# A graph layer with a mixture of experts on one core: when two late experts' weights, two sets of scatters and a few transposes are issued

## The chip, the cores and the metric

The kernel runs on one core of one Trainium2 chip. The metric is device time in microseconds (us) of one launch, as the median of several runs. The core has five engines that run side by side, each with its own queue of instructions in a fixed order: TensorE (PE in the profile, with PEld for its weight loads), VectorE (DVE), ScalarE (ACT), GpSimd (POOL) and SyncE (SP). An engine waits with the instruction at the head of its queue, and everything behind that instruction waits with it. DMAs are issued from the queues of SP, ACT and POOL and run on 16 DMA engines that all three share.

## What is computed

`x` is 3125 nodes of 256 floats, `src` and `dst` are 100,000 edges sorted by `dst`. All numbers are float32.

```
xn  = layernorm(x)
e   = relu((xn[dst] - xn[src]) @ theta.T + theta_b + xn[src] @ phi.T + phi_b)
gnn = segment_max(e, dst)                       # 0 where a node has no edge
mix = linear attention of xn over 8 heads, projected, + bias
x   = x + gnn + mix
z   = layernorm(layernorm(x))
top 2 of 8 experts per node, by softmax(z' @ Wr);  expert: gelu(z @ W1 + b1) @ W2 + b2
out = x + w0 * expert0(z) + w1 * expert1(z)
```

An expert has two matrices, 256 by 1024 and 1024 by 256, 1 MB each.

## The kernel before, in words

**Edges.** The message of an edge is a maximum over rows of a table `b_d` in DRAM. The edges lie in 128 runs of 782. POOL gathers 128 rows at a time (`gather`, L107, tile `g`), 755 of these steps, and DVE folds each into a running maximum (`fold`, L366). Eight steps share a window `g` of the pool `wide`, which has `WN` = 5 buffers. SP stores each folded window to `s_d`. The order of steps is cut into four groups of node tiles: group 0 has tiles 12 to 24, group 1 tiles 5 to 11, group 2 tiles 1 to 4, group 3 tile 0.

**A group** (`group`, L1128) starts when its last fold is in the queue: `carry` links the 128 runs, `routed_tile` finishes the gnn sum, both norms and the router for each node tile, `dispatch` works out each node's slots in the experts' buffers and scatters the nodes' rows there (`xs_d`, L114, two scatters a tile). Then the `Stream` (`go`, L720) takes the experts' lots: load rows (`rows`), transpose (`turn`, L698), scale (`scaled`, L709, tile `xe`), and a unit of eight steps: `hp` (L615), GELU into `hT` (L617), and, one unit behind, `yp` (L639). Group 0 has 16 units, groups 1 and 2 have eight each. Weights come in four parts of 512 KB on ACT's queue, three experts' worth of buffers `w`.

**Group 3** is one tile, and all its 128 nodes go through all eight experts (`dense_tile`, L786), in the order 5, 6, 7, 0, 1, 2, 3, 4. The first three experts' weights are still held by the stream. Expert 0 is loaded into parts of `xn_lo` (SP, in `first_maxima`) and `xn_hi` (ACT's queue, at the end of `go`). Expert 1 goes into two buffers of `wide` (SP, in `combines`). Experts 2, 3 and 4 take the freed buffers `w` (ACT's queue, `next_dense`, L1199, 2 MB in one DMA), issued at step 1 of the third, fourth and fifth expert. DVE makes the scaled input `xe` of the next expert (L802) at step 1 of each expert, and adds each expert's result (L829).

**The combines** (`combine`, L1295; `finale`, L1334) bring the experts' rows of groups 0, 1 and 2 back: POOL gathers `ys_d` into a buffer of `wide` (two gathers a tile, four tiles), DVE adds them with two operations a tile (L1308), and SP stores `out`. There are seven: four tiles from each of tiles 12, 16, 20, one tile 24, then 5 (four), 9 (three) and 1 (four). The text calls them c12, c16, c20, c24, c5, c9, c1. A buffer of `wide` can be used again when its `out` store has landed.

**The maxima** (`first_maxima`, L1207) find, for the four first nodes, the maximum over all nodes that have an edge to them: DVE, L1228, 25 steps beside the folds, then PE transposes (L1235) and two more small stages (L1242, `last_ends`, L1264 and L1275). **The last fold** of group 3 is followed on PE by `pick_ends` (L1287) and `carry` (L373, L384), then by `routed_tile(0)` (L445 to L495).

**What sets the order.** The order on PE, DVE, ACT and SP is the order in which Python emits it, written by generators: `yield 3` means that the task goes on three ticks later. A tick is one POOL instruction (`TICK` = 1.25 us); each issue on POOL moves the clock by one. A stream unit's steps follow a second count, `clock["pe"]`, of the work that PE has been given. An engine runs ahead of the ticks when its operands are there, so ticks fix orders, not times.

Of the kernel before, what the change touches and what calls it, by code (L numbers as in the profile page):

```python
# [19 lines left out]
P = 128  # L20
# [12 lines left out]
FC = H // P  # L33
# [34 lines left out]
def gps_layer(ctx: ExitStack, tc: tile.TileContext, x, src, dst, thetaT, phiT, gbias, wq, wkvT,  # L68
# [583 lines left out]
    class Stream:  # L652
# [67 lines left out]
        def go(self):  # L720
            units = Units(self.ps, self.act)
            u, q = 0, -1
            for k in range(3):
                self.next_w(k)
                yield 25
            while True:
                if u == len(self.lots):

                    for _ in units.last():
                        yield room()  # L730
                    units.behind = None
                    if not self.open:
                        break
                    if G - 3 in self.through:
                        nc.scalar.activation(table, eps, AF.Sqrt)
                    while u == len(self.lots):
                        yield 1
                if ("xe", u) not in self.held:
                    self.rows(u // 2)
                    yield 8  # L740
                    self.turn(u)
                    yield 2
                    self.scaled(u)
                    yield 2
                g, e, h = self.lots[u]
                v = u // 2
                if u % 2 == 0:
                    ys = self.at(2) if v % 2 else self.act.tile([P, 4, D], F32, name="ys", bufs=1)

                def done(r, yp, u=u, ys=ys):  # L750
                    g, e, h = self.lots[u]
                    n = self.half(u)
                    nc.tensor.matmul(yp[0:n, :], ident[0:E, e:e + 1].to_broadcast([E, n]), b2_sb, start=False, stop=True)  # L753
                    nc.scalar.copy(ys[0:n, u % 2 * 2 + r, :], yp[0:n, :])
                    if u % 2 and r:
                        move(nc.scalar, self.two(ys_d, u // 2), self.as_two(ys, u // 2))
                        if u + 1 == len(self.lots) or self.lots[u + 1][0] != g:
                            self.through.add(g)

                between = {4: lambda: self.turn(u + 1), 6: lambda: self.scaled(u + 1)}  # L760
                if u % 2 == 0:
                    between[1] = lambda: self.rows(v + 1)
                if h == 0:
                    q += 1
                    if q:
                        between[7] = lambda: (self.next_w(q + 2, self.parts), self.part())
                at_step = dict(between)
                for f in (0, 2, 5):
                    between[f] = lambda f=f: (self.part(), at_step.get(f, int)())
                w1t, w2t = self.held["w", q]  # L770
                for _ in units.run(e, w1t, self.held["xe", u], w2t, done, between, 2, self.half(u)):
                    yield room()
                u += 1
            for k in range(3):
                dense_w[DENSE[k]] = self.held["w", q - 2 + k]
            dense_half(0, 1, xn_hi[:, 0:FC, :].rearrange("p i d -> p (i d)"), nc.scalar)
            clock["through"] = True

    def spread(pool, i, pick):
# [6 lines left out]
    def dense_tile(act, ps, mm, i, shared, w, next_w, order=range(E), ready=None):  # L786


        tr = mm.tile([P, 2, P], F32, name="mm")
        for c in range(2):  # L790
            nc.tensor.transpose(tr[:, c, :], xn2(i)[:, c * P:(c + 1) * P], ident)
        xT = act.tile([P, 2, P], F32, name="xT", bufs=1)
        nc.vector.tensor_copy(xT, tr)
        held = {}
        yield 1

        def scaled(k):
            if k < E:
                e = order[k]
                held["xe", e] = act.tile([P, 2, ROWS], F32, name="xe")  # L800
                for c in range(2):
                    nc.vector.tensor_scalar(held["xe", e][:, c, 0:P], xT[:, c, :], sm[:, c, e:e + 1],  # L802
                                            sm[:, 2 + c, e:e + 1], op0=OP.mult, op1=OP.add)

        while ready is not None and "through" not in ready:
            yield 1
        scaled(0)
        o = act.tile([P, D], F32, name="o", bufs=1)

        def second_bias():  # L810

            bt_p = mm.tile([E, P], F32, name="mm")
            nc.tensor.transpose(bt_p, full, ident)
            bt = act.tile([E, P], F32, name="bt", bufs=1)
            nc.vector.tensor_copy(bt, bt_p)
            held["bt"] = bt

        def add_bias():
            bb = mm.tile([P, D], F32, name="mm")
            nc.tensor.matmul(bb, held["bt"], b2_sb, start=True, stop=True)  # L820
            nc.vector.tensor_add(x_sb[:, i, :], x_sb[:, i, :], bb)

        units = Units(ps, act, True)
        for k, e in enumerate(order):
            def done(r, yp, k=k, e=e):
                if k == 0:
                    nc.vector.tensor_scalar(o, yp, full[:, e:e + 1], None, op0=OP.mult)
                else:
                    nc.vector.scalar_tensor_tensor(o, yp, full[:, e:e + 1], o, op0=OP.mult, op1=OP.add)  # L829

            between = {1: lambda k=k: scaled(k + 1)}
            if k == 1:
                between.update({3: second_bias, 5: add_bias})
            if k > 1:
                between[1] = lambda k=k: (next_w(k - 2), scaled(k + 1))
            while k == 1 and not shared:
                yield 1
            for _ in units.run(e, w[e][0], held["xe", e], w[e][1], done, between, 1, P):
                yield 1
        nc.vector.tensor_add(o, o, x_sb[:, i, :])  # L840
        for _ in units.last():
            yield 1
        n = rows_in(i)
        move(nc.sync, out[i * P:i * P + n, :], o[0:n])
# [263 lines left out]
    def dispatch(g, half, i0, i1, top, top_i, taken):  # L1108

        ro = at_hand["route"]  # L1110
        while not all(i in routed for i in range(i0, i1)) or len(taken) < half:
            yield 1
        yield 1
        made = []
        at = i0 - GROUPS[g][0]
        rest = shares(ro, i0, i1, top[:, at:at + i1 - i0, :], top_i[:, at:at + i1 - i0, :], made,
                      15 if g == G - 2 and half == 0 else 0)
        start(rest, clock["now"] + next(rest))
        yield from slots(ro, mm, g, half, i0, i1, made[0], taken)
        yield 1 if g == G - 2 else 9  # L1120
        put = []
        for i in range(i0, i1):
            n = rows_in(i)
            for k in range(2):
                put.append((xs_d[g][:], slot_i[0:n, k, i:i + 1], xn2(i)[0:n]))
        scatter(*put)
# [80 lines left out]
    def first_maxima():  # L1207
# [11 lines left out]
        for i in range(NT):  # L1219
# [4 lines left out]
            for k in range(FIRST):  # L1224
# [4 lines left out]
                                                   op1=OP.max)  # L1229
                yield 1.4  # L1230
        most = at_hand["first"].tile([P, 2, FIRST], F32, name="most")
        for c in range(2):
            tr = mm.tile([P, FIRST, P], F32, name="mm")
            for k in range(FIRST):
                nc.tensor.transpose(tr[:, k, :], of_k[:, k, c * P:(c + 1) * P], ident)  # L1235
            on_pe(1.2)
            yield 4
            nc.vector.tensor_reduce(most[:, c, :], tr, AX.X, OP.max)
            yield 2
# [75 lines left out]
    def combines(g):  # L1315

        i0, i1 = GROUPS[g]
        whole = i1 - (i1 == NT)
        for i in range(i0, whole, W // 2):
            nt = min(W // 2, whole - i)  # L1320
            start(combine(g, i, nt))
            yield 2 * nt
            if g == 0 and i == i0 + W // 2:

                while "shared" not in clock:
                    yield 1
                yield 6
                for k in range(2):
                    dense_half(1, k, wide.tile([P, HALF], F32, name="g"))
        if i1 == NT:  # L1330
            start(combine(g, NT - 1, 1))
            yield 2

    def finale():  # L1334

        for g in range(G - 1):
            while g not in at_hand["ffn"].through:
                yield 1
            yield from combines(g)

    def starts(g):

# [7 lines left out]
    def folding():  # L1350

        for g in range(G):
            last = None
            rows = s_d[1 + P * COL[g]:1 + P * COL[g + 1], :].rearrange("(p t) d -> p t d", t=STEPS[g])
            for w, (t0, n) in enumerate(starts(g)):
# [6 lines left out]
                if g < G - 1 or t0 + n < STEPS[g]:  # L1362
                    move(nc.sync, rows[:, t0:t0 + n, :], wins[g, w][:, 0:n, :])
            clock["last"] = last
            if g == 0:
                open_late()
            start(group(g))
# [193 lines left out]
```

## Time and profile before

| | us |
|---|---|
| median of 3 runs (lowest, highest) | 1219.15 (1218.51, 1221.02) |
| the profiled execution, its own time | 1217.85 |
| its span, first to last instruction | 1216.0 |
| mean granted TensorE clock | 0.856 of full speed |
| busy: PE, DVE, ACT, POOL | 938.2, 678.6, 326.0, 885.8 |

Some stretches, from the view of busy time by stage (busy us of each engine; granted clock; DMA engines' mean busy share):

| stretch, us | what runs | PE | DVE | POOL | clock | DMA |
|---|---|---|---|---|---|---|
| 550 to 600 | group 0's units | 50.00 | 18.45 | 38.12 | 1.00 | 0.82 |
| 850 to 900 | group 1's units | 50.00 | 26.14 | 38.41 | 1.00 | 1.01 |
| 950 to 1000 | group 2's routing | 22.84 | 38.87 | 37.77 | 0.50 | 0.55 |
| 1050 to 1100 | group 2's units | 48.02 | 21.14 | 37.95 | 0.97 | 1.02 |
| 1100 to 1150 | last fold, tile 0 | 48.84 | 25.00 | 34.90 | 1.00 | 0.65 |
| 1150 to 1216 | dense experts, combines | 52.39 | 24.26 | 24.06 | 0.93 | 0.63 |

A line of a timeline gives start, duration, engine, line, operation, output from input with its shape, a count, and in brackets the idle time before it and what ended that time. "issue" there means that the profile shows no engine or DMA that was waited for.

### The profile page before, as it was taken

How to read it: one execution, taken by the hardware profiler on the slowest of the kernel's cores; microseconds unless marked ns; L12 is line 12 of the kernel's file. 1: busy time of each engine (PE TensorE's matmuls, PEld its weight loads, DVE VectorE, ACT ScalarE, POOL GpSimd, SP SyncE). 2: the span in 40 equal slices, each digit the busy share in tenths (PEclk: the TensorE clock that was granted, in tenths of full speed). 3: DMA queues.
4: the chain of work that ended last, by engine and by line, in shares of the span. 5: the costliest groups of instructions: out<-in, count | busy, mean ns of one | idle time of the engine just before them, and what ended most of it. 6: DMA issues, size and time to landing. Idle time of an engine off the chain costs nothing.

```text
span 1216.0 us, 13364 instructions
## 1 busy us (share of the span) xinstructions
PE 938.2 (77%) x3929; PEld 670.4 (55%) x3929; DVE 678.6 (56%) x1998; ACT 326.0 (27%) x762; POOL 885.8 (73%) x911
## 2 busy tenths in 40 slices
PE   6556866645923548689999999979999527999986
PEld 5323433323311323258888887868887315777786
DVE  7669866685336772433333587455546764433633
ACT  4212222210101222133333343323332112332331
POOL 6677777777777777777777777777777777776733
PEclk9778888866965557889999999989999557999998
DMA  8668877666685664467888787689999658998683
GB/s 280 214 200 277 302 253 242 227 227 207 207 292 194 239 235 157 156 238 258 285 307 310 251 284 271 227 308 356 380 370 367 219 191 305 375 387 301 201 338 94
DMA packets 103928, 320.13 MB, mean 263 GB/s; under 512 B 20897, under 2 KB 44186, under 8 KB 92325
## 3 DMA queue, kind: packets, MB, share of 16 engines
q0 software_dynamic: 44032, 119.73, 31.5%
q1 hardware_dynamic: 29724, 115.08, 24.4%
q10 hardware_dynamic: 30089, 84.36, 19.3%
q8 instruction: 33, 0.54, 0.2%
q14 instruction: 50, 0.41, 0.1%
HBM read 192.05 MB, written 127.04 MB: 262 GB/s over the span
## 4 chain that ended last, share of the span: by engine, by line
PE 43%; DMA 5%; issue 4%; POOL 3%; DVE 2%; ACT 1%; ACTq 0%; POOLq 0%; DVEq 0%; SPq 0%
PE yp L639 18%; PE hp L615 18%; PE yp L753 3%; POOL g L107 2%; DMA w<-in_w 2%; DMA g<-b_d,srcI 2%; PE trf L698 1%; POOL xs_d L114 1%; DMA xn_lo<-b_d 1%; PE am L445 1%; DVE g L366 1%; PE mm L491 0%; DMA xn_hi<-xs_d 0%; DMA r<-s_d,end_i 0%; PE mm L403 0%
## 5 line engine op out<-in xcount | busy, mean ns | idle before, releaser
L107 POOL DMA_INDIRECT g<-b_d,srcI x755 | 738.2, 978 | 238.4 <-issue 203.8
L366 DVE SCALAR_TENSOR_TENSOR g<-g,cut 128x256 f32<-128x256 f32 x751 | 363.5, 484 | 356.8 <-DMA g<-b_d,srcI 339.0
L639 PE MATMUL yp<-w,hT 128*128 128x256 f32 (+1 forms) x1120 | 296.8, 387 | 0.0
L615 PE MATMUL hp<-xe,w 128*128 128x256 f32 (+2 forms) x1216 | 285.9, 361 | 11.5 <-issue 5.6
L615 PEld LDWEIGHTS hp<-xe,w 128*128 128x128 f32 x1216 | 216.7, 196 | 49.2 <-issue 18.0
L617 ACT ACTIVATE hT<-hp,sm 128x256 f32<-128x256 f32 (+2 forms) x320 | 140.2, 439 | 335.8 <-PE hp L615 335.3
L639 PEld LDWEIGHTS yp<-w,hT 128*128 128x128 f32 (+1 forms) x1120 | 201.1, 185 | 39.7 <-issue 12.4
L1012 PE MATMUL kv<-wkv,xn_lo 128*128 128x512 f32 x96 | 54.5, 720 | 38.0 <-DVE kn L1030 24.1
L1012 PE MATMUL kv<-wkv,xn_hi 128*128 128x512 f32 x104 | 59.3, 724 | 30.9 <-DVE kn L1030 30.2
L107 POOL DMA_INDIRECT g<-ys_d,from_i x48 | 46.1, 960 | 32.4 <-DVE g L1308 18.7
L445 PE MATMUL am<-cr,oh 128*128 128x257 f32 x86 | 37.3, 560 | 27.8 <-DVE r L450 19.9
L1012 PEld LDWEIGHTS kv<-wkv,xn_lo 128*128 128x128 f32 x96 | 21.1, 231 | 63.8 <-issue 60.3
L1012 PEld LDWEIGHTS kv<-wkv,xn_hi 128*128 128x128 f32 x104 | 22.8, 230 | 58.3 <-issue 55.6
L1228 DVE SCALAR_TENSOR_TENSOR xn_lo<-xn_lo,no_edge 128x256 f32<-128x256 f32 x96 | 45.9, 479 | 16.1 <-DMA xn_lo<-b_d 16.1
L401 PE MATMUL mm<-bias,ones 1*128 1x512 f32 x50 | 32.4, 731 | 16.2 <-ACT x_sb L408 12.9
L753 PE MATMUL yp<-b_sb,ident 8*128 8x256 f32 (+1 forms) x128 | 43.9, 422 | 0.0
L1016 ACT ACTIVATE sq<-kv 128x1024 f32<-128x1024 f32 x25 | 25.5, 1019 | 59.3 <-PE kv L1012 59.3
L445 PEld LDWEIGHTS am<-cr,oh 128*128 128x128 f32 x86 | 20.3, 267 | 37.1 <-issue 24.9
L709 ACT ACTIVATE xe<-trf,sm 128x256 f32<-128x256 f32 (+1 forms) x64 | 31.3, 544 | 27.6 <-PE trf L698 27.6
L1035 PEld LDWEIGHTS dots_p<-kn,vn 128*128 128x128 f32 x200 | 26.9, 199 | 19.0 <-issue 19.0
L1024 ACT ACTIVATE rsk<-var,eps 128x16 f32<-128x16 f32 x25 | 7.7, 308 | 110.7 <-DVE var L1021 110.7
L698 PE MATMUL trf<-ident,xn_hi 128*128 128x128 f32 (+1 forms) x128 | 19.2, 275 | 22.2 <-DMA xn_hi<-xs_d 22.2
(285 smaller groups left out, 991.1 us busy)
## 6 DMA issues: line engine op xcount, KB each, us to landing
s_d<-g SPq DMA_DIRECT2D x80, 1024.0 KB
w<-in_w ACTq DMA_DIRECT2D x84, 512.0 KB
w<-in_w ACTq DMA_DIRECT2D x6, 2048.0 KB
g<-b_d,srcI POOLq DMA_INDIRECT x755, 4.5
s_d<-g SPq DMA_DIRECT2D x13, 896.0 KB
xn_hi<-xs_d ACTq DMA_DIRECT2D x12, 512.0 KB
xs_d<-zero ACTq DMA_DIRECT2D x8, 512.0 KB
b_d<-bt SPq DMA_DIRECT2D x5, 640.0 KB
```

What stands on the lines that cost most here:

```text
L107: got = nc.gpsimd.indirect_dma_start(out=to, out_offset=None, in_=table, in_offset=row_index(index))
L366: nc.vector.scalar_tensor_tensor(g[:, j, :], last, cut[:, t:t + 1], g[:, j, :], op0=OP.add, op1=OP.max)
L401: nc.tensor.matmul(am, ones[0:1, :], bias, start=True, stop=False)
L445: nc.tensor.matmul(r2, picks[k], carried[g], start=(k == 0), stop=(k == len(slices) - 1))
L615: nc.tensor.matmul(hp[:, 0:n], w1t[:, c, f, :], xe[:, c, 0:n], start=(c == 0), stop=(c == 1))
L617: nc.scalar.activation(hT[f][:, 0:n], hp[:, 0:n], AF.Gelu, bias=sm[:, 4 + f, e:e + 1])
L639: nc.tensor.matmul(yp[r][0:part, :], hT[q][:, r * part:(r + 1) * part], w2t[:, q, :], start=(q == 0), stop=(q == FC - 1 and self.whole))
L698: nc.tensor.transpose(tr[:, c, r * n:(r + 1) * n], self.held["xs", u // 2][0:n, u % 2 * 2 + r, c * P:(c + 1) * P], ident[0:n, 0:n])
L709: nc.scalar.activation(xe[:, c, 0:n], self.held["tr", u][:, c, 0:n], AF.Identity, bias=sm[:, 2 + c, e:e + 1], scale=sm[:, c, e:e + 1])
L753: nc.tensor.matmul(yp[0:n, :], ident[0:E, e:e + 1].to_broadcast([E, n]), b2_sb, start=False, stop=True)
L1012: nc.tensor.matmul(kv[:, k, :], xnT(i, c), wkv[:, c, k * INNER:(k + 1) * INNER], start=(c == 0), stop=(c == 1))
L1228: nc.vector.scalar_tensor_tensor(of_k[:, k, :], b, no_edge[:, k, i:i + 1], of_k[:, k, :], op0=OP.add, op1=OP.max)
```

## The change

There are five edits.

1. **Weights of experts 1 and 0.** The two loads of expert 1 and the second load of expert 0 (1 MB each) leave their places in `combines` and at the end of `go`. A new task `more_weights` issues all three from SP one tick after the last fold of group 3 is emitted; the third waits for a mark that the stream sets before its last unit. A `memset` of one column on DVE stands before each load. The wait for `shared` and six ticks in `combines`, after the second combine, go with it.
2. **Scatters** of groups 0 and 1: 14 ticks after their slots instead of 9.
3. **Maxima:** eight more ticks between the last maximum (L1228) and the first transpose (L1235).
4. **First unit of group 2:** 3, 1 and 1 ticks between rows, transposes, scaling and the unit, instead of 8, 2 and 2.
5. **First `xe` of the dense tile** is made right after its transposes; before, it waited until the stream had emitted its last step.

```
@@ Stream.go
                 if ("xe", u) not in self.held:
+                    soon = self.lots[u][0] == G - 2
                     self.rows(u // 2)
-                    yield 8
+                    yield 3 if soon else 8
                     self.turn(u)
-                    yield 2
+                    yield 1 if soon else 2
                     self.scaled(u)
-                    yield 2
+                    yield 1 if soon else 2
...
                 w1t, w2t = self.held["w", q]
+                if u + 1 == len(self.lots) and not self.open:
+                    clock["last lot"] = True
                 for _ in units.run(e, w1t, self.held["xe", u], w2t, done, between, 2, self.half(u)):
...
             for k in range(3):
                 dense_w[DENSE[k]] = self.held["w", q - 2 + k]
-            dense_half(0, 1, xn_hi[:, 0:FC, :].rearrange("p i d -> p (i d)"), nc.scalar)
             clock["through"] = True
@@ dense_tile
         nc.vector.tensor_copy(xT, tr)
         held = {}
-        yield 1
...
+        if ready is not None:
+            while "last lot" not in ready:
+                yield 1
+        scaled(0)
+        yield 1
         while ready is not None and "through" not in ready:
             yield 1
-        scaled(0)
@@ dispatch
         yield from slots(ro, mm, g, half, i0, i1, made[0], taken)
-        yield 1 if g == G - 2 else 9
+        yield 1 if g == G - 2 else 14
@@ first_maxima
         most = at_hand["first"].tile([P, 2, FIRST], F32, name="most")
+        yield 8
         for c in range(2):
@@ combines
             start(combine(g, i, nt))
             yield 2 * nt
-            if g == 0 and i == i0 + W // 2:
-
-                while "shared" not in clock:
-                    yield 1
-                yield 6
-                for k in range(2):
-                    dense_half(1, k, wide.tile([P, HALF], F32, name="g"))
@@ new
+    def more_weights():
+        for k in range(2):
+            to = wide.tile([P, HALF], F32, name="g")
+            nc.vector.memset(to[:, 0:1], 0.0)
+            dense_half(1, k, to)
+        while "last lot" not in clock:
+            yield 1
+        to = xn_hi[:, 0:FC, :].rearrange("p i d -> p (i d)")
+        nc.vector.memset(to[:, 0:1], 0.0)
+        dense_half(0, 1, to)
@@ folding
             clock["last"] = last
+            if g == G - 1:
+                start(more_weights(), clock["now"] + 1)
             if g == 0:
```

## The prediction

> **What bounds the kernel now.** I read the chain of waits first, then the timeline of each engine around every edit, then busy time by stage. The chain names TensorE:
>
> ```profile
> PE 43%; DMA 5%; issue 4%; POOL 3%; DVE 2%; ACT 1%; ACTq 0%; POOLq 0%; DVEq 0%; SPq 0%
> PE yp L639 18%; PE hp L615 18%; PE yp L753 3%; POOL g L107 2%; DMA w<-in_w 2%; DMA g<-b_d,srcI 2%; PE trf L698 1%; POOL xs_d L114 1%; DMA xn_lo<-b_d 1%; PE am L445 1%; DVE g L366 1%; PE mm L491 0%; DMA xn_hi<-xs_d 0%; DMA r<-s_d,end_i 0%; PE mm L403 0%
> ```
>
> The timeline says where it is PE and where not. Until the last edge gather (1114.62) POOL paces: 0.95 us a gather and 0.30 between. Beside this, from 1007.8 on, PE has more unit work than it gets through, so that a loss there pushes all behind it. From 1122 to 1140 a chain of small steps (tile 0) decides, then eight dense experts on PE and the seven combines (c12, c16, c20, c24, c5, c9, c1). Three places carry my sum.
>
> PE, group 2's first unit (start, duration, what; in brackets the idle time before):
>
> ```profile
> 1018.41 1.03 PE L639 MATMUL yp<-w,hT 128*88 128x256 f32 x4
> 1021.10 0.33 PE L1235 MATMUL mm<-ident,xn_lo 128*128 128x128 f32 x1 [1.66 <-DVE xn_lo L1228]
> ...
> 1024.82 0.48 PE L1235 MATMUL mm<-ident,xn_lo 128*128 128x128 f32 x1 [1.02 <-DVE xn_lo L1228]
> 1025.09 1.38 PE L615 MATMUL hp<-xe,w 128*128 128x176 f32 x4
> ```
>
> PE stands at the maxima's transposes for VectorE, with units behind. After it, four `hp` take 1.38 instead of 0.76 (at 1017.81).
>
> PE, where the fold has ended and where the dense tile begins:
>
> ```profile
> 1122.36 2.75 PE L1287 MATMUL am<-g,xn_lo 128*128 128x256 f32 x12
> ...
> 1140.36 1.16 PE L615 MATMUL hp<-xe,w 128*128 128x128 f32 x8
> ```
>
> The fold's last work on DVE ended at 1120.05, but L1287 began at 1122.36 with no idle time before: PE was behind. Between the lines lie 10.2 us of stream units, which end at 1140.36.
>
> The tail, PE and then DVE:
>
> ```profile
> 1187.52 1.19 PE L615 MATMUL hp<-xe,w 128*128 128x128 f32 x4 [5.59 <-issue]
> ```
>
> ```profile
> 1186.15 0.48 DVE L1308 SCALAR_TENSOR_TENSOR g<-g,share,x_sb 128x256 f32<-128x256 f32 x1 [3.57 <-DMA g<-ys_d,from_i]
> ...
> 1187.08 0.60 DVE L802 TENSOR_SCALAR xe<-xT,sm 128x128 f32<-128x128 f32 x2
> ```
>
> PE's 5.59 has no releaser, but DVE shows it: the input of the seventh expert stands behind c9's first pair of gathers. POOL says why these come late:
>
> ```profile
> 1165.72 0.94 POOL L107 DMA_INDIRECT g<-ys_d,from_i  x1 [10.80 <-DVE g L1308]
> ...
> 1182.22 0.94 POOL L107 DMA_INDIRECT g<-ys_d,from_i  x1 [6.81 <-DVE g L1308]
> ```
>
> The named DVE work was long done. What ended last is the store of `out` that frees the buffer: c5 waits for c16's (issued 1153.27, so 12.4 us), c9 for c20's (issued 1164.66, 17.5 us).
>
> I call the start of the dense tile's first `hp` T (1140.36) and count the tail from there: weights of experts 2, 3, 4 are issued at T+14.9, 22.0, 29.0; the last `yp` ends at T+68.07.
>
> **Part by part**, against the profiled execution's own 1217.85 (span 1216.0). The median of the runs, 1219.15, is 1.30 above.
>
> *Scatters.* Nothing is added; two waits go:
>
> ```profile
> 747.15 1.18 POOL L114 DMA_INDIRECT xs_d<-xn_lo,slot_i  x1 [1.77 <-issue]
> ...
> 774.99 1.01 POOL L114 DMA_INDIRECT xs_d<-xn_lo,slot_i  x1 [1.17 <-ACT hT L617]
> ```
>
> Over the usual 0.30 these are 1.47 and 0.87, so POOL gains 2.3. Each tick is one gather of 1.25, so the streams of groups 0 and 1 start about 6.25 later. The cover: after group 1's stream PE idles 4.08 before L373 (943.62) and 5.08 before L384 (949.39), then 16.75 for group 2's rows (1006.38). Group 2's first gather of edge sums waited 0.65 for stores, so I count 1.0 as lost again: **-1.3**, bounds 0 and -2.3. With the cover gone it would cost up to 6.25; 25.9 of idle time excludes that.
>
> *Maxima.* Between 1018.41+1.03 and 1025.09 lie 5.65 us, of which the transposes need 0.44 beyond what overlaps; the half clock after it (L615 1.38, L639 1.91 instead of 1.03) costs 1.8. Eight ticks later the last maximum is done, and with the units seven ticks earlier the transposes come 15 ticks later among them. What is late next are L1242 to L1275; they end before 1117, and are needed at 1122. **-7.0**, bounds 0 (the stall moves) and -7.4.
>
> *First unit of group 2, seven ticks earlier.* 7 x 1.25 = 8.75 us of unit work move before the last fold's steps in PE's queue; of the 10.2 us behind, about 2.5 stay, so 7.7 come ahead. The unit's real start is fixed by its rows (16.75 of waiting), so nothing begins sooner; the wait moves into PE's queue, and behind it stand only group 2's routing, done by then, and the units.
>
> L1287 then comes at 1122.36 - 1.3 - 7.0 + 7.7 = 1121.8; the fold ends at 1120.05 - 1.3 = 1118.75, so it still waits for PE. From L1287 to the dense tile's transposes (L791, 1135.94) there are 13.6; with the unit work gone some 1.2 of waits behind units go, so 12.4: L791 at 1134.2. The copy (0.42), four L802 (1.11) and the handovers make 1.6 if `xe` is made at once (edit 5; before, two small stages came first): first `hp` at 1135.8 instead of 1140.36: **-4.5**. PE now idles about 3.5 before it. Group 2's rows show a price: after 1.99 idle (1096.36) the next `yp` took 1.62 instead of 1.03. I take **+0.7**, bounds 0 and +1.8 (the maxima's). [...]
>
> *Weights.* The loads leave ACT's queue and c16's place: 3 MB now go at about 1118 to 1130 instead of 1143 to 1158.
>
> ```profile
> 1120.00:1130.00 10.00, 9.48 (x47) 7.34 (x46) 3.28 (x12) 1.58 (x4) 7.58 (x8) 1.00 0.33 93
> 1130.00:1140.00 10.00, 9.96 (x47) 6.31 (x46) 7.08 (x34) 1.71 (x4) 7.59 (x8) 1.00 0.36 105
> 1150.00:1160.00 10.00, 10.00 (x66) 8.85 (x65) 4.74 (x12) 4.01 (x11) 3.19 (x4) 1.00 1.06 428
> ```
>
> The last two columns are the DMA engines' share and GB/s: a third busy where the loads go, full where they were. At 410 GB/s they need 7.7 us, and expert 1 is first used at T+5.9, some 11 after 1130. The three `memset`s (one of one column, L388, took 0.06) stand on DVE ahead of the fold's successors; their buffers are those of windows stored some 40 us earlier: 0, bounds 0 and +2 (a wait there holds up tile 0). The third load waits on SP for the stream's rows to be read, with `out` stores behind that come 15 us later: 0.
>
> *Tail.* The combines start about five ticks earlier in the order and `scaled` about three, so the `xe` of expert seven stands behind all three pairs of c9 (before: one), that of expert eight behind all four of c1 (before: two). A pair is 2 x 1.255 = 2.5 on POOL. c16's store (T+15.0) lands in the lull after expert 2's load, at T+23.2; c5's eight gathers end at T+33.3. c20's store (T+22.0) shares with experts 3 and 4: before, it landed 2.4 after expert 4's load. I take that again: T+38 (before, T+41.9). Six gathers: third pair landed T+47.6, seventh expert T+48.1 (before 47.16). c1's gathers from T+45.5, its last pair lands T+57.7, eighth expert T+58.3 instead of 57.34: **+0.9**. Bounds: c20's store lands at T+31 (below), or later than before (below). [...]
>
> Sum: -4.5 (which holds scatters, maxima and order) + 0.7 + 0.9 = -2.9; 1217.85 - 2.9 = 1214.95, and + 1.30 = **1216.2**.
>
> **Rivals.**
>
> *B, faster.* With 3 MB out of the way each expert's load takes 5 us of 7 and leaves a lull; c20's store lands in that of T+29 to 31. c9 then follows c5 at once (T+33.3), c1 from T+40.8, last pair T+53.3, eighth expert T+53.8: 4.5 earlier than A: 1211.7. For it: 0.48 MB went on SP's queue around 1170 to 1174, in such a lull. Against it: the store was complete only at 1182.2 all the same.
>
> *C, no change.* The weight wait of group 2 (1096.36: 1.99 idle and slow clock after it, 4.0 in all; a part issued at 1081.21 took 15.02) comes twice, since PE now runs 7 ahead of the parts and the DMA engines are full from 1010 to 1110 (share 0.98 and 1.01): 1216.2 + 4.0 = 1220.2. Against it: the parts are issued by PE's progress, so they move too.
>
> *D, slower.* The `xe` behind whole combines: if c20's store needs 21.5 us instead of 16, c9 starts at T+43.5, every pair and the eighth expert come 5.5 later, and a seventh expert 5 us later leaves PE about 1.0 more of slow clock: 1216.2 + 6.5 = 1222.7. It decides from a start of c9 at T+42.4 on. For it: 17.5 us before, with only part of the expert loads beside it, and the expert loads now start earlier after the store. Against it: less is queued.
>
> **Numbers.** A (forecast) 0.36, own range 1214 to 1218.5; B 0.30; C 0.15; D 0.19. A measurement of this kernel tells about 0.2% (2.4 us) from no change, so faster is below 1216.7 and slower above 1221.6. Faster: B and 0.6 of A, 0.51; slower: D and a little of C, 0.20; same: 0.29. The range goes from 1210.5 (B less the bounds of scatters and clock) to 1222.5 (D).
>
> **What would show it.** L1235 without idle time before it and no half clock after; L114's at 0.30; L1287 near 1121.8, first dense `hp` near 1135.8; DMA share near 0.9 at 1118 to 1130; POOL's waits before c5 and c9, and DVE's place of the last two L802. It is wrong if the `memset`s wait, if a weight wait appears in 1010 to 1110, or if c9 starts far from T+38.

## The result and the profile after

| us | before | after |
|---|---|---|
| median of 20 runs (lowest, highest) | 1220.72 (1214.38, 1229.87) | 1220.70 (1216.25, 1228.06) |
| profiled execution, own time | 1217.85 | 1223.43 |
| its span | 1216.0 | 1221.6 |

The ratio is 1.0003, 95% interval 0.9986 to 1.0020. No difference is measured; in us the interval is -1.7 to +2.4. The three runs of before that the prediction started from (median 1219.15) are among its twenty here. The runs of one kernel lie up to 15.5 us apart, and the profiled execution of after is 2.7 above its median, that of before 2.9 below. So the two traces must not be compared by their spans. They are compared by stretches, each counted from an event that both have.

**POOL.** The start of each edge gather in after, less that of the same gather in before, is +4.27 us at the 290th (441 us), where no edit has acted yet: that is chance. It is +3.35 at 627 us, +0.51 at 790 us and +1.49 at the last edge gather. Of the step of 2.8 between 627 and 790 us, 2.3 lie between 726 us (+2.82) and 789 us (+0.50), at the scatters of group 1; the other moves are smaller, and chance as far as the traces show. POOL's timeline of after (start, duration; in brackets the idle time before and what ended it):

```profile
755.02 1.01 POOL L114 DMA_INDIRECT xs_d<-xn_lo,slot_i  x1 [0.30 <-issue]
...
782.02 1.00 POOL L114 DMA_INDIRECT xs_d<-xn_lo,slot_i  x1 [0.30 <-ACT hT L617]
...
1116.11 0.95 POOL L107 DMA_INDIRECT g<-b_d,srcI  x1 [0.30 <-issue]
...
1165.96 0.94 POOL L107 DMA_INDIRECT g<-ys_d,from_i  x1 [11.90 <-DMA out<-g]
...
1179.80 0.94 POOL L107 DMA_INDIRECT g<-ys_d,from_i  x1 [4.15 <-DVE g L1314]
```

The scatters' waits are gone: 0.30 is POOL's usual step. The last two lines are c5's and c9's first gathers.

**PE up to the dense tile.** Its timeline of after (the maxima's transposes are L1241 now, `pick_ends` is L1293):

```profile
1048.62 0.60 PE L1241 MATMUL mm<-ident,xn_lo 128*128 128x128 f32 x4
...
1089.74 0.54 PE L615 MATMUL hp<-xe,w 128*128 128x176 f32 x2 [0.34 <-DMA w<-in_w]
...
1123.07 2.75 PE L1293 MATMUL am<-g,xn_lo 128*128 128x256 f32 x12
...
1135.50 0.69 PE L482 MATMUL mm<-ident,xt 128*128 128x128 f32 x2 [5.28 <-ACT xt L471]
1135.98 0.63 PE L793 MATMUL mm<-ident,xn_lo 128*128 128x128 f32 x2
1136.65 0.59 PE L489 MATMUL mm<-br_sb,ones 1*128 1x8 f32 x2
1137.17 1.02 PE L491 MATMUL mm<-wr_sb,xtT 128*128 128x8 f32 x4
1138.05 6.42 PE L615 MATMUL hp<-xe,w 128*128 128x128 f32 x36
```

The transposes wait for nothing. The weight wait that was 1.99 is 0.34. The first dense `hp` (T = 1138.05) comes 21.94 us after the last edge gather instead of 25.74: 3.8 gained.

**The early weights.** Busy time by stage of after (stretch and its length, then PE, PEld, DVE, ACT and POOL with their numbers of instructions; the last three columns are the granted clock, the DMA engines' share and GB/s):

```profile
1120.00:1130.00 10.00, 9.48 (x44) 6.89 (x43) 3.80 (x17) 0.84 (x2) 7.63 (x8) 1.00 0.80 300
1130.00:1140.00 10.00, 4.69 (x21) 4.04 (x20) 7.06 (x34) 1.71 (x4) 7.58 (x8) 0.55 0.69 248
1150.00:1160.00 10.00, 10.00 (x70) 9.44 (x70) 8.41 (x21) 4.04 (x11) 3.14 (x4) 1.00 0.70 191
```

The 3 MB go where the DMA engines were a third busy (0.33 and 0.36 in before), and no product waits for them. The clock column has 0.55 in 1130 to 1140 us, where PE idles before T; in before it has 1.00 there.

**The tail** gives it back. From T to the end of the last `yp` it took 68.07 us before and takes 75.71 now. PE stands still three times; its timeline of after:

```profile
1179.19 1.19 PE L615 MATMUL hp<-xe,w 128*128 128x128 f32 x4 [6.13 <-issue]
...
1189.94 0.70 PE L615 MATMUL hp<-xe,w 128*128 128x128 f32 x4 [2.01 <-issue]
...
1200.12 1.19 PE L615 MATMUL hp<-xe,w 128*128 128x128 f32 x4 [2.90 <-issue]
```

These are the sixth, seventh and eighth expert. PE's lines name no cause; DVE's timeline of after does:

```profile
1150.07 0.42 DVE L826 TENSOR_TENSOR x_sb<-x_sb,mm 128x256 f32<-128x256 f32 x1 [2.10 <-PE mm L825]
1150.40 0.48 DVE L1314 SCALAR_TENSOR_TENSOR g<-g,share,x_sb 128x256 f32<-128x256 f32 x1
...
1154.06 0.48 DVE L1314 SCALAR_TENSOR_TENSOR g<-g,share 128x256 f32<-128x256 f32 x1
1154.46 0.60 DVE L803 TENSOR_SCALAR xe<-xT,sm 128x128 f32<-128x128 f32 x2
...
1172.64 0.48 DVE L1314 SCALAR_TENSOR_TENSOR g<-g,share,x_sb 128x256 f32<-128x256 f32 x1 [9.61 <-DMA g<-ys_d,from_i]
...
1178.35 0.48 DVE L1314 SCALAR_TENSOR_TENSOR g<-g,share 128x256 f32<-128x256 f32 x1 [0.68 <-DMA g<-ys_d,from_i]
1178.75 0.60 DVE L803 TENSOR_SCALAR xe<-xT,sm 128x128 f32<-128x128 f32 x2
...
1189.10 0.48 DVE L1314 SCALAR_TENSOR_TENSOR g<-g,share 128x256 f32<-128x256 f32 x1 [0.79 <-DMA g<-ys_d,from_i]
1189.50 0.60 DVE L803 TENSOR_SCALAR xe<-xT,sm 128x128 f32<-128x128 f32 x2
...
1199.28 0.48 DVE L1314 SCALAR_TENSOR_TENSOR g<-g,share 128x256 f32<-128x256 f32 x1 [0.81 <-DMA g<-ys_d,from_i]
1199.68 0.60 DVE L803 TENSOR_SCALAR xe<-xT,sm 128x128 f32<-128x128 f32 x2
```

Read it backwards from the sixth expert's input. That input (1178.75) stands in DVE's queue behind two pairs of c5 (1172.64 to 1178.35), which wait for their gathers. These started at 1165.96, when c16's `out` store had landed. That store could only be issued after c16's last sum (1154.06 + 0.48, T+16.5), and c16's sums stand behind the dense tile's bias (L826, 1150.07), though their gathers were issued by 1142. Expert 2's load, 2 MB, was issued at 1153.48 (T+15.4), ahead of the store.

The inputs of the seventh and eighth expert (1189.50, 1199.68) stand behind pairs of c9 and c1 in the same way, and have another source. c9's first gather (1179.80) came 4.15 us after c5's last gather, so it did not wait for c5. It waited for its buffer, that is for c20's store. That store was issued at T+22.4 and reports its landing in 16 parts. By the trace's semaphore records 15 of them were in by T+35.8 and the last at T+41.0 (before: 14 by T+34.8, the others at T+40.8 and T+41.1). c9 started 0.8 after that last part, and the same 0.8 lie between c16's last part (T+27.1) and c5's start. DVE, which the line names, ended an addition of c5 at about that moment.

All twelve runs below fell on chips that held TensorE back (mean granted clock 0.74 to 0.76 against 0.84 to 0.86; the kernel before took 1738 to 1765 us there), so their ratios are compared with each other only, and their traces by order and by time from T. Ratios are taken over the fast runs of each kernel (those within 1.5% of its fastest), and three of the profiles (experiment 1's first, experiment 3's second, the second edit alone) are of slower runs.

### The profile page after: what moved, and what is told of

It is laid out like the page before. It is cut to its first block, busy times and chain, and to the rows that moved or that the text cites. A ratio compares the mean times of both kernels' runs of the same rounds, so it can differ in the third digit from the quotient of the medians.

```text
span 1221.6 us, 13377 instructions
## 1 busy us (share of the span) xinstructions
PE 955.4 (78%) x3929; PEld 679.2 (56%) x3929; DVE 679.2 (56%) x2001; ACT 326.6 (27%) x762; POOL 888.9 (73%) x911
## 4 chain that ended last, share of the span: by engine, by line
PE 40%; DMA 25%; POOL 17%; issue 8%; DVE 8%; ACT 1%; POOLq 0%; DVEq 0%; SPq 0%; ACTq 0%
DMA g<-b_d,srcI 21%; POOL g L107 16%; PE yp L639 14%; PE hp L615 14%; DVE g L366 3%; PE mm L403 2%; PE yp L754 2%; PE bp L241 2%; DMA w<-in_w 2%; PE mm L401 1%; POOL xs_d L114 1%; PE trf L698 1%; PE am L445 1%; DMA r<-s_d,end_i 1%; PE mm L491 1%
## 5 line engine op out<-in xcount | busy, mean ns | idle before, releaser
L615 PE MATMUL hp<-xe,w 128*128 128x256 f32 (+2 forms) x1216 | 289.3, 365 | 14.3 <-issue 11.0
L615 PEld LDWEIGHTS hp<-xe,w 128*128 128x128 f32 x1216 | 220.7, 200 | 51.8 <-issue 21.3
L617 ACT ACTIVATE hT<-hp,sm 128x256 f32<-128x256 f32 (+2 forms) x320 | 140.4, 439 | 334.1 <-PE hp L615 333.7
L1017 PE MATMUL kv<-wkv,xn_hi 128*128 128x512 f32 x104 | 58.3, 712 | 28.9 <-DVE kn L1035 28.7
L107 POOL DMA_INDIRECT g<-ys_d,from_i x48 | 46.4, 966 | 30.1 <-issue 12.2
L445 PE MATMUL am<-cr,oh 128*128 128x257 f32 x86 | 37.1, 559 | 27.7 <-DVE r L450 18.6
L445 PEld LDWEIGHTS am<-cr,oh 128*128 128x128 f32 x86 | 20.3, 267 | 36.5 <-issue 23.2
L401 PE MATMUL mm<-bias,ones 1*128 1x512 f32 x50 | 36.6, 818 | 3.2 <-ACT xtT L486 3.2
L1040 PEld LDWEIGHTS dots_p<-kn,vn 128*128 128x128 f32 x200 | 26.7, 197 | 20.5 <-issue 20.5
```

The lines of the kernel that those rows point to most:

```text
L107: got = nc.gpsimd.indirect_dma_start(out=to, out_offset=None, in_=table, in_offset=row_index(index))
L401: nc.tensor.matmul(am, ones[0:1, :], bias, start=True, stop=False)
L445: nc.tensor.matmul(r2, picks[k], carried[g], start=(k == 0), stop=(k == len(slices) - 1))
L615: nc.tensor.matmul(hp[:, 0:n], w1t[:, c, f, :], xe[:, c, 0:n], start=(c == 0), stop=(c == 1))
L617: nc.scalar.activation(hT[f][:, 0:n], hp[:, 0:n], AF.Gelu, bias=sm[:, 4 + f, e:e + 1])
L1017: nc.tensor.matmul(kv[:, k, :], xnT(i, c), wkv[:, c, k * INNER:(k + 1) * INNER], start=(c == 0), stop=(c == 1))
```

## The experiments

Two explanations of the tail are set against each other. Order theory: the inputs of the last experts stand on DVE behind sums whose rows are late. Transfer theory: stores and expert loads set the tail, whatever DVE's order.

**1. Sums of the last three combines later**, three times:

```
-        yield 10
+        yield 10 if g == 0 else 22
```

> The changed kernel with one number more: the sums of c5, c9 and c1 are put into VectorE's queue 22 ticks after their gathers instead of 10; gathers, stores and loads keep their places. Order theory (the inputs of experts six to eight stand on VectorE behind sums whose rows are late): the three stops of PE in the tail (6.1, 2.0 and 2.9 us in the changed kernel) go, and from the dense tile's first product to the last store it takes about 66 us instead of 76.6; the kernel is 8 to 10 us faster than the changed one, about 1211. Transfer theory (expert loads and stores of out on the DMA engines set the tail, whatever the order): c5 and c9 start no earlier, the stops turn up at other places, at most 2 us are gained, about 1219.

> The changed kernel with the sums of c5, c9 and c1 22 ticks after their gathers instead of 10. Order theory: the three stops of PE in the tail (6.1, 2.0 and 2.9 us in the changed kernel) go, from the dense tile's first product to the last store it takes about 66 us instead of 76.6, and the kernel is 8 to 10 us faster than the one before. Transfer theory: c9 starts no earlier than 41.7 us after the dense tile's first product, the stops turn up at other places, and it is at most 2 us faster.

> The changed kernel with the sums of c5, c9 and c1 22 ticks after their gathers instead of 10, looked at once more. Order theory: the three stops of PE in the tail (6.1, 2.0 and 2.9 us in the changed kernel) go, from the dense tile's first product to the last store it takes about 66 us instead of 76.3. Transfer theory: c9 starts no earlier than 41.7 us after that product and the stops turn up at other places.

Ratios to the kernel before 0.984 (0.973 to 0.995) and 0.978 (0.967 to 0.990); the third is a single run of each kernel (1731.29 against 1746.78 us). The order came out as meant: DVE no longer waits for a gather anywhere after T, in all three profiles. In after these waits are 25.0 us, but in the changed kernel on these chips (experiment 5) only 2.6, so there was little to take away. The sixth expert's input is made at T+28.4 to T+29.0 (after: T+40.7, experiment 5: T+40.5). But T to the last `yp` took 83.8 to 84.6 us, against 83.4 in experiment 5, so the expected 66 (counted to the last store, which is later still) failed. DVE's timeline of the first of them shows what took the place:

```profile
1659.38 0.75 DVE L803 TENSOR_SCALAR xe<-xT,sm 128x128 f32<-128x128 f32 x2
1684.83 0.48 DVE L834 SCALAR_TENSOR_TENSOR o<-yp,full,o 128x256 f32<-128x256 f32 x1 [24.70 <-remote]
1685.23 0.59 DVE L803 TENSOR_SCALAR xe<-xT,sm 128x128 f32<-128x128 f32 x2
```

DVE now waits 24.70 for PE's result, and ACT and PE stop in the middle of the experts. Two lines of ACT's timeline of the same run:

```profile
1680.27 0.37 ACT L617 ACTIVATE hT<-hp,sm 128x128 f32<-128x128 f32 x1 [9.10 <-remote]
1689.16 0.62 ACT L617 ACTIVATE hT<-hp,sm 128x128 f32<-128x128 f32 x2 [8.52 <-remote]
```

"remote" is a releaser that the profile doesn't know. Such stops lie all over these executions: 302.5 us of them at L617 in experiment 5. They hide what DVE's order is worth. What was seen is what the transfer theory expected: c5 and c9 start no earlier than in experiment 5, and the stops turn up at other places. But these stops have no known releaser, so they can't be put down to transfers either.

**2. Sums of the first four combines earlier**, so that c16's stand ahead of the bias:

```
-        yield 10
+        yield 6 if g == 0 else 10
```

> The changed kernel with the sums of c12, c16, c20 and c24 6 ticks after their gathers instead of 10, so that c16's sums stand ahead of the bias of the dense tile and its store is issued before expert 2's load. Order theory alone (only the queue order of late sums counts): inputs of experts six to eight stand behind as many pairs as in the changed kernel, but the pairs come earlier if the buffers do; c5 starts at 17 to 20 us after the dense tile's first product instead of 27.9, the stop before the sixth expert goes, 4 to 8 us faster than the changed kernel. Transfer theory: the store of c16 is still held up by the expert loads and c5 starts at 25 or later; within 2 us of the changed kernel.

Ratio 0.990 (0.982 to 0.998). Here the trace is clear. c5's first gather in the changed kernel (POOL's timeline, experiment 5, T = 1628.72):

```profile
1655.74 0.94 POOL L107 DMA_INDIRECT g<-ys_d,from_i  x1 [13.24 <-DMA out<-g]
```

and with the earlier sums (T = 1624.91; the second line is c9's first):

```profile
1641.32 0.95 POOL L107 DMA_INDIRECT g<-ys_d,from_i  x1 [2.79 <-DVE g L1314]
1653.79 0.95 POOL L107 DMA_INDIRECT g<-ys_d,from_i  x1 [2.44 <-DMA out<-g]
```

T+16.4 instead of T+27.0: 10.6 us, because the first four combines' sums stand earlier, c16's eight of them by 5 us. Experiment 1's first run, on the same chip and with these sums in the old place, has T+27.5. T to the last `yp`: 78.6 us instead of 83.4. In the ratio the expected 4 to 8 us do not show (0.983 for the changed kernel there, with overlapping intervals).

**3. Both**, twice: `yield 6 if g == 0 else 22`.

> Both of the above: sums of the first four combines 6 ticks after their gathers, those of the last three 22. Order theory: no stop of PE in the tail above 0.5 us, 65 us or less from the first dense product to the last store, about 1210, a little better than the late sums alone or equal to them. Transfer theory: as the early sums alone.

> The changed kernel with the sums of c12, c16, c20 and c24 6 ticks after their gathers instead of 10, and those of c5, c9 and c1 22 ticks. Order theory: c16's store goes out ahead of the dense tile's bias, c5 starts about 18 us after the first dense product instead of 27.9, no stop of PE in the tail above 0.5 us where the changed kernel has 6.1, 2.0 and 2.9, 65 us or less from that product to the last store instead of 76.3: 8 to 11 us faster than the kernel before. Transfer theory: c5 starts at 25 us or later and the time is within 2 us of the changed kernel's.

Ratios 0.987 (0.970 to 1.004) and 0.978 (0.963 to 0.993). c5 starts at T+17.0 and T+17.3, DVE waits for no gather, and T to the last `yp` is 70.9 and 75.2 us: the shortest of all runs there, and above the expected 65, with stops of PE of up to 2.95 where at most 0.5 were expected.

**4. The change without the early weights** (first edit undone whole; two places of it are shown), twice:

```
+                for k in range(2):
+                    dense_half(1, k, wide.tile([P, HALF], F32, name="g"))
...
-            if g == G - 1:
-                start(more_weights(), clock["now"] + 1)
```

> The changed kernel without its first edit: the loads of expert 1 and of the second half of expert 0 are back in their old places; the other four edits stay. VectorE's queue then has the inputs of experts six, seven and eight behind no pair of c5, all of c5 and all of c9, which is less than in the changed kernel. Order theory: the front keeps its gain (first dense product about 22 us after the last edge gather, instead of 25.7) and the tail loses less than in the changed kernel: 3 to 6 us faster than it, about 1215 to 1218. Transfer theory (3 MB out of the way is worth something by itself): 2 to 5 us slower than the changed kernel.

> The changed kernel without its first edit: loads of expert 1 and of the second half of expert 0 in their old places. VectorE's queue then has the inputs of experts six, seven and eight behind no pair of c5, all of c5 and all of c9. Order theory: the front keeps its gain (first dense product about 22 us after the last edge gather instead of 25.7) and the tail loses less than in the changed kernel: 3 to 6 us faster than the kernel before. Transfer theory: c16's store waits for the 3 MB again, 2 to 5 us slower than the changed kernel and so than the kernel before.

Ratios 0.992 (0.984 to 0.999) and 0.981 (0.972 to 0.989), so the same kernel differs by 1% between two chips, and neither is told from the changed kernel's 0.983. c5 starts at T+27.2 and T+27.7, against T+27.0 in experiment 5, so 2 MB in front of c16's store on SP's queue make no difference when that store is late anyway. Neither theory's expected time (3 to 6 us faster, or 2 to 5 slower) is seen.

**5. The changed kernel itself there**

> The changed kernel itself, beside the kernel before, on the chips on which the earlier runs of this study took 1742 to 1756 us for the kernel before. If every part is long there (TensorE held back), the front's gains on PE (fewer waits of queued unit work) should count at least as much as in the first comparison, and the late sums cost the same stops: order theory, 0.5 to 1.5% faster than the kernel before, and slower than its versions with later or earlier sums (ratios 0.978 to 0.990). If the sums' place in VectorE's queue is of no account, its ratio is that of those versions, 0.98 to 0.99.

Ratio 0.983 (0.976 to 0.991). So with TensorE held back the change is faster by 1.7%, and no version above can be told from it by its time. That is what was expected if the sums' place in DVE's queue is of no account there; the order theory expected it to be slower than the versions with moved sums.

**6. Third and fourth edits alone**

> The kernel before with the third and fourth edits alone (maxima's transposes eight ticks later, first unit of group 2 seven ticks earlier). The transposes wait for nothing (before: 1.66, 0.48, 0.95 and 1.02 us), and the unit work behind the last fold shrinks from 10.2 us to some 2.5. VectorE's queue comes out with the inputs of experts six to eight behind no pair of c5, all of c5, all of c9. Order theory: faster than the kernel before by 3 to 6 us and faster than the changed kernel. Rival (the gain comes from the weights): no difference to the kernel before.

Ratio 1.015 (1.009 to 1.022): the expectation failed. T comes 78.0 us after the last gather (changed kernel there: 54.2; edits 1 and 2 alone: 72.9 and 69.2). What makes it slower than before is not settled; before has no trace from these chips.

**7. Second edit alone, and first edit alone**

```
-        yield 1 if g == G - 2 else 9
+        yield 1 if g == G - 2 else 14
```

> The kernel before with the second edit alone: scatters of groups 0 and 1 14 ticks after their slots instead of 9. In the runs of this study TensorE is held back, and even the changed kernel's scatters of group 1 wait 26.0 and 19.6 us on POOL; five ticks are 6.25 us for each of four sets of scatters. Scatter theory (the changed kernel's 0.983 there comes from this edit, against the 1.015 of the third and fourth alone): 0.965 to 0.985 of the kernel before. Rival (it comes from the early weights): within 0.5% of the kernel before.

> The kernel before with the first edit alone: the 3 MB for experts 1 and 0 go out behind the last fold. VectorE's queue comes out with the input of expert six behind all four pairs of c5, of seven behind all of c9 and of eight behind all of c1, more than in the changed kernel. Order theory: VectorE's waits for gathers stand ahead of the inputs of experts six to eight, these inputs are made at 38 us, 48 us and 60 us or later after the first dense product (before: 28.0, 46.7, 56.9), and the time is no better than the kernel before's, 0 to 1% worse. Transfer theory (3 MB out of the way of the stores is worth something by itself): c5's and c9's gathers start 3 to 8 us earlier than 25.4 and 41.9, and the kernel is 0.2 to 0.5% faster.

Scatters: 0.991 (0.985 to 0.996), faster, by less than expected. POOL's timeline of experiment 6, without later scatters, and then of this one:

```profile
1045.39 1.18 POOL L114 DMA_INDIRECT xs_d<-xn_lo,slot_i  x1 [32.53 <-ACT hT L617]
```

```profile
1073.65 1.17 POOL L114 DMA_INDIRECT xs_d<-xn_lo,slot_i  x1 [22.56 <-issue]
```

Five ticks are 6.25 us, and this wait is 10.0 shorter. The sum of POOL's waits at L114 is 93.0 us, against 101.8 in experiment 6 and 99.6 with edit 1 alone, each in one profile. Of the parts that were run alone this edit is the only one that was faster. The fifth edit was not run alone.

Weights: 1.006 (0.998 to 1.013). c5 and c9 start at T+17.4 and T+34.7, 8.0 and 7.2 earlier than in the trace of before. Yet the inputs of the sixth, seventh and eighth expert are made at T+34.8, 51.5 and 62.5, later than before's 28.0, 46.7 and 56.9, though the mean granted clock differs between these two (0.750 and 0.856). Each theory is met in part. The transfers come earlier, as the transfer theory expected, but its gain in time is not seen. The last two inputs and the time are as the order theory expected; the sixth input came before the expected T+38.

**What decides c5's start**, over all profiles (us from T; last sum of c16 on DVE, issue of expert 2's load on ACT, first gathers of c5 and c9 on POOL, end of the last `yp`):

| kernel | c16's last sum | expert 2's load | c5 | c9 | last yp |
|---|---|---|---|---|---|
| before | 12.9 | 14.9 | 25.4 | 41.9 | 68.1 |
| after | 16.5 | 15.4 | 27.9 | 41.8 | 75.7 |
| after, experiment 5 | 16.9 | 15.8 | 27.0 | 37.0 | 83.4 |
| late sums (3) | 16.5 to 17.0 | 15.4 to 16.0 | 27.1 to 27.5 | 37.1 to 37.5 | 83.8 to 84.6 |
| early sums | 11.9 | 15.6 | 16.4 | 28.9 | 78.6 |
| both | 12.2, 12.5 | 15.9, 16.2 | 17.0, 17.3 | 29.0, 35.3 | 70.9, 75.2 |
| without early weights | 16.8, 17.0 | 15.7, 15.9 | 27.2, 27.7 | 37.2, 41.1 | 83.5, 79.7 |
| edits 3 and 4 | 16.9 | 15.8 | 26.7 | 41.1 | 76.9 |
| edit 1 | 12.5 | 14.6 | 17.4 | 34.7 | 79.5 |
| edit 2 | 11.2 | 14.9 | 18.1 | 35.9 | 78.7 |

In every run in which c16's last sum, and so its store, comes after expert 2's load is issued, c5 starts at 26.7 or later. Where it comes 2 us or more ahead, c5 starts by 18.1. Before is the one exception (12.9, but 25.4).

The DMA packets in the traces show why. c16's store has 512 packets of 1 KB, an expert's load 128 of 16 KB. In after none of the 512 ended before T+20.7 and only 16 by T+23, while expert 2's packets ran from T+16.4 on. With the earlier sums (experiment 2) all 512 had ended by T+15.3, ahead of expert 2's first packet (T+16.6). In before 2 MB of expert 1's weights, issued 6.6 us ahead of the store on the same queue, ran until T+17.6; 431 of the 512 got through by T+19, and the last ended at T+24.2, beside expert 2's. The weights ahead of the store are not enough by themselves: they stood there in edit 2 alone too, ran until T+15.6, and the store was through at T+17.0.

So neither theory holds alone. DVE's order (bias ahead of c16's sums) sets when the store goes out; the load that has then started holds it up; and DVE's order again (inputs behind c5, c9, c1) hands the delay to PE. The first two links are shown by experiment 2, in which nothing but the order changes, and by the packets. The last one is read from the traces: taking it away (experiment 1) removed DVE's waits, but its worth in time couldn't be seen under the other stops. What holds the last part of c20's store, and so c9, until T+41.0 in after was not tested.

## Why the prediction came out as it did

- **No change instead of -2.9 us** (1216.2 from the 1219.15 of the first three runs; -4.5 from the 1220.72 of all twenty). The time lies in the stated range (1210.5 to 1222.5), but outside the likeliest case's own (1214 to 1218.5). The front came out a little better than forecast (-2.8 - 3.8 = -6.6 instead of -4.5, some of it chance), the tail far worse. That the sum is nothing is luck: the loss in the tail happens to cancel the gain ahead of it.
- **Scatters, forecast -1.3.** Right in kind: both waits went, and POOL's offset falls by their 2.3 where they were. The 1.0 that I gave back to group 2's edge sums was not lost there (that wait is 0.71 instead of 0.65). From the 290th gather to the last the offset falls by 2.8 in all; what goes beyond 2.3 is chance as far as the traces show.
- **Maxima and unit order.** L1293 came 6.96 after the last gather; the forecast's 1121.8 with a last gather at 1113.32 is 8.48. The 1.5 more fits the weight wait, which shrank from 1.99 to 0.34, where rival C had it come twice. C's number (1220.2) is the nearest of all to the measured 1220.70, but its mechanism is wrong: that is luck. The maxima's stall went without moving elsewhere, and the granted clock stays at 1.00 from 1015 to 1131 us, where before it was 0.50 from 1021.9 to 1028.8 and from 1097.0 to 1100.4.
- **The chain after the fold.** From L1293 to L793 12.91 (forecast 12.4), from there to T 2.07 (1.6). From the last gather to T 21.94, forecast 22.48: the front was right. PE's idle time was 5.28, not 3.5; the first expert took 6.25 instead of 5.78, +0.5 (forecast +0.7). This does not reach the end, since the sixth expert waits for its input anyway.
- **Weights.** Right: no wait at the `memset`s (0.07 and 0.06), none at expert 1. I had expert 1 used from T+5.9 on; it is the fifth in order and came at T+27.8, so the margin was larger than I said.
- **The tail, forecast +0.9, measured +7.6** (75.71 - 68.07). This step failed, and in three terms of it. First, "c16's store (T+15.0) lands in the lull after expert 2's load, at T+23.2": it was issued at T+16.5, behind that load, landed at T+27.1, and c5 started at T+27.9. I had also left out that two pairs of c5 stand ahead of the sixth input, so that PE stops three times instead of twice. Second, c20's store: I took 16 us for it (T+22.0 to T+38); it was issued at T+22.4 and c9 started at T+41.75, 19.3 later, because of one late part of 16. Without that part c9 would have followed c5's last gather at T+37.9, an estimate from c5's start and eight gathers of 1.25. The seventh and eighth expert began at T+51.9 and T+62.1 instead of T+48.1 and T+58.3, 3.8 late, which is c9's delay handed on. Third, the clock: it was granted at 0.50 from 1175.4 to 1182.3 and from 1199.3 to 1206.1, at the stops of 6.13 and 2.90 us, and from the eighth expert's first `hp` to the last `yp` it took 13.6 instead of 10.7, 2.9 more, for which the forecast had nothing. 0.9 + 3.8 + 2.9 = 7.6. How much of this the first term caused by way of the others, no run separates.
- **Rival D** named the second of these waits. Its price, 6.5, is near the 6.7 beyond the forecast, but not for its reason: its condition (c9 from T+42.4 on) was missed by 0.65, it had c9 5.5 late instead of 3.8, and the rest of the 6.7 is the clock of the eighth expert. **B** failed: c20's store missed the lull too.
- **The sum.** -2.8 - 3.8 + 7.6 = +1.0 us, inside the measured -1.7 to +2.4. The profiled pair differs by 5.6; the rest is the 4.3 of chance before the first edit and 0.3 after the last `yp`.

## What to carry to other kernels

When work is brought forward, write down what each in-order queue then holds ahead of the next critical instruction, one by one: here PE waited for an input behind additions that waited for rows, whose buffer waited for a store. Look for thresholds: a 512 KB store issued 3.7 us before a 2 MB load freed its buffer after 4.5 us (experiment 2), one issued 1.1 us after it took 11.4 (after). A lead of 2.0 us was enough with nothing ahead of the store on its queue (edit 1 alone, 4.8 us), and not with 2 MB ahead of it (before, 12.4). And where a stop on one engine has no releaser, read the queue of the engine that makes its operand.

## What the hardware showed that I had not expected

- A stop of 2.01 us on PE (1189.94) left the granted clock at 1.00 (`hp` 0.70), one of 2.90 (1200.12) came with 0.50 (`hp` 1.19), and so did one of 1.99 in the kernel before (1096.36, next `yp` 1.62). The length alone doesn't decide. The clock fell at 1199.3 in after, 2.1 into the stop of 2.90, and at 1097.0 in before, 0.7 after the stop of 1.99 had ended. In the clock records of these two traces it is either 1.00 or 0.50, and each stretch of one value, but for the last of each trace, lasts a whole multiple of 3.41 us (in after it changes at 1175.4, 1182.3, 1199.3 and 1206.1). Why one stop came with 0.50 and another of the same length did not is not shown.
- On the chips that held TensorE back, ACT and PE stopped again and again with a releaser unknown to the profile, ACT for up to 27.9 us (experiment 4's first run, at 397 us), and one kernel's ratio moved by 1% from chip to chip. What an edit is worth there need not be what it is worth elsewhere: the same change gave 0.983 there and 1.000 in the first comparison. What the version with both sums moved would give at the clock of the first comparison (0.84 to 0.86) was not measured.
